# Causal attention with group norm on one core: diagonal blocks packed in pairs, with the tokens of odd blocks reversed

## The chip, the core and the metric

The kernel runs on one core of a Trainium2 chip. The metric is the device time of one execution in microseconds, which the program's own core sets. An execution is repeated, and a median is given with the lowest and highest value.

## What is computed

The input x has 32 images of 256 channels and 32 x 32 pixels. An image is treated as 1024 tokens of 256 channels. It is group normalized (32 groups of 8 channels, no scale or offset), projected to queries, keys and values, and goes through attention of 8 heads with 32 channels each; the result is added to x. The mask is strictly causal: token q sees only keys k < q, and token 0 sees none. All is float32.

```
q = q_w @ xn + q_b;  k, v = kv_w @ xn + kv_b          # xn = group_norm(x), per image
scores = q.T @ k / sqrt(32)                            # per head, 1024 x 1024
scores = where(k < q, scores, -10000)
attn = where(k < q, softmax(scores), 0)
out = x + (attn @ v).T
```

## The kernel before

**Layout.** Scores are held with keys on the 128 partitions and queries along the columns. The 1024 tokens make 8 blocks of 128. The work is done for a group g of 4 heads at a time (two groups an image) and for two halves of 512 queries. Only the blocks on and below the diagonal are computed. The exps are not divided by their sum: the value product takes the raw exps, the sums over keys are made apart, and the division comes last.

**Steps.** An image is 12 steps, 6 for each head group (`visits`). A step makes the scores of one "full" piece, 512 columns for each of 4 heads, and one "half" piece of 256 columns. The product has 32 rows (one head's channels) and 64 columns (half a block of keys), so 8 tiles of TensorE's array work beside each other (L285). The scores of a step go to three PSUM buffers `sT` of two banks each, of which the pool has three in all: two for the full piece, two heads each, and one for the half piece. ScalarE takes the exps out of them: two of 128 x 1024 into the tile `e` (L348), then one of 128 x 1024 into `eh` (L346), always in this order. The scores of the next step can begin when the exps have emptied these buffers. A piece that lies on the diagonal is masked in place by GpSimd with an affine select (L301), for 4 heads and one or two blocks at once; the half pieces of steps 0 and 5 and the full pieces of steps 0, 1, 4 and 5 lie on it. The columns above the diagonal inside a block are computed, exponentiated and then set to zero.

**What else is in a step.** After its scores a step has one projection stage for the next image (L158, into `pp` or `ppv`; L238 and L254 copy it out with ScalarE), and then the value products of the step before (L373, into `acc`). VectorE adds up the exps of all key blocks in place, for the sums over keys (L381): within one head group one 512-wide and one 1536-wide sum twice, a 2048-wide one twice, and six 1024-wide ones. Those tiles are then folded across partitions by accumulating DMAs that GpSimd issues (L397), stacked, summed and inverted, and spread again (SP's DMAs). `finish` multiplies the numerators with the inverses (L483), adds the bias and x (L484), writes token 0 (L486), and stores; it runs four times an image, in steps 1, 1, 2 and 3 of the second image after it.

**The next image.** Its norm is prepared in between. `norm_channels`, `norm_mean`, `norm_deviation` (L186 to L188, VectorE) and `norm_variance` (L200, ScalarE) come in the steps before. `norm_rstd` belongs to step 4: GpSimd makes the power −1/2 (L208) and the shift (L210). `norm_apply` (L224, ScalarE: x times rstd plus shift into `xn`, 512 columns each) comes at the end of steps 5, 6, 7 and 9. The first projection that reads `xn` comes in step 7.

**What sets the order.** The kernel runs in a manual schedule for TensorE, ScalarE, VectorE and GpSimd: each engine has its instructions in the order in which the program writes them, and the framework adds the waits. In each step the program writes the scores with their exps and masks, then what is entered for that step in `at` (projections, folds), then the value products and key sums of the step before, then what is entered in `after` (norm, finish). Two lines enter the work on the next image; the numbers are steps relative to the first step of that image:

```
PROJECT = (-5, -4, -3, -2, -1, 0, 1, 2, 3, 4, 5, 6)
PREPARE = (-16, -15, -9, -9, -8, -8, -7, -6, -5, -3)
```

The last two entries −8 of PREPARE are `norm_variance` and `norm_rstd`, and the four after them `norm_apply`. So GpSimd's queue holds, in this order: the mask of step 4, the power, the shift, the masks of step 5, a fold, and the masks of the next head group's step 0, which is step 6. ScalarE's holds: the exps of step 5, a projection's copy, the first `norm_apply`, the exps of step 6.

Of the kernel before, what the change touches and what calls it, by code (L numbers as in the profile page):

```python
# [28 lines left out]
WIDE = 64  # L29
# [3 lines left out]
def tile_norm_attention_residual(  # L33
# [65 lines left out]
    def unshifted():  # L99
# [24 lines left out]
        def load_weights():  # L124
            for n, w in enumerate((q_w, kv_w[0:C], kv_w[C : 2 * C])):
                live["wn", n] = epool.tile([P, 4, HALFBANK], F32, tag="eh", bufs=4, name=f"wn_{n}")[:, :NG, :C]
                nc.sync.dma_start(out=live["wn", n], in_=w.rearrange("(o p) c -> p o c", p=P))
# [33 lines left out]


# [49 lines left out]
        def norm_apply(b, hf, g):  # L212

            if (hf, g) == (0, 0):
                live["xn", b] = work.tile([P, NG, S], F32, tag="xn", name=f"xn_{b}")
            cols = slice(hf * HALF, (hf + 1) * HALF)
            xn, xt = live["xn", b][:, g, cols], live["x", b][:, g, cols]
            rstd = live["rstd", b][:, g : g + 1]
            if (b, hf, g) == (0, 0, 1):
                nc.scalar.activation(xn, live["less_mean"], AF.Identity, scale=rstd)  # L220
            elif b == 0:
                nc.vector.tensor_scalar(xn, xt, live["minus_mean", b][:, g : g + 1], rstd, ALU.add, ALU.mult)
            else:
                nc.scalar.activation(xn, xt, AF.Identity, bias=live["shift", b][:, g : g + 1], scale=rstd)  # L224

        def project_qk(b, g, n, hf):
# [6 lines left out]
            for cc in range(NG):  # L233
                product(
                    pp, wT[:, cc, n * C + g * P : n * C + (g + 1) * P], live["xn", b][:, cc, cols],
# [6 lines left out]
        def project_v(b, n):  # L242
# [4 lines left out]
            pp = spare(f"ppv_{b}_{n}").rearrange("p (s c) -> p s c", c=C)  # L247
            for s in range(2):
                for cc in range(NG):
                    product(  # L250
                        pp[:, s, :], live["xn", b][:, cc, (2 * n + s) * P : (2 * n + s + 1) * P],
                        wT[:, cc, 2 * C : 3 * C], start=cc == 0, stop=cc == NG - 1,
                    )
# [12 lines left out]
        def piece(g, hf, k, part=None):  # L266
            d = k - hf * BPH
            if d == 1:

                blocks = [(k, slice(P, HALF), slice(P, HALF)), (k + 2, slice(0, P), slice(3 * P, HALF))]  # L270
            elif d == 2:
                blocks = [(k, slice(0, HALFBANK), slice(HALFBANK, HALF))]
            elif part is not None:
                blocks = [(k, slice(0, HALFBANK), slice(part * HALFBANK, (part + 1) * HALFBANK))]
            else:
                blocks = [(k, slice(0, HALF), slice(0, HALF))]
            return g, hf, k, part, tuple(blocks)

        def scores_of(pc, pair, j, n=0):

            b, (g, hf, k, part, blocks) = pc
            rows = slice(HD * j, HD * (j + 1))
            kb, cols, of = blocks[n]
            return [
                nc.tensor.matmul(  # L285
                    pair[c : c + WIDE, cols], lhsT=live["k", b, g][rows, kb * P + c : kb * P + c + WIDE],
                    rhs=live["q", b, g][rows, hf * HALF + of.start : hf * HALF + of.stop],
                    start=True, stop=True, skip_group_check=True,
                )
                for c in range(0, P, WIDE)  # L290
            ]

        def mask(pc, e, heads=slice(0, 4)):


            g, hf, k, part, blocks = pc
            if k < hf * BPH:
                return
            n = len(blocks)
            diagonal = e[:, heads, : n * P].rearrange("p j (n q) -> p j n q", q=P)  # L300
            nc.gpsimd.affine_select(  # L301
                out=diagonal, in_=diagonal, pattern=[[0, heads.stop - heads.start], [0, n], [1, P]],
                compare_op=ALU.is_gt, fill=0.0, base=0, channel_multiplier=-1,
            )
            if k == 0:
                nc.gpsimd.memset(e[0:1, heads, 0:1], 1.0)

        def scores(b, full, half):


            tag = "e0" if full[2] == 0 else "e"
            name = f"{b}_{full[0]}_{full[1]}_{full[2]}"
            e = epool.tile([P, 4, HALF], F32, tag=tag, bufs=4 if tag == "e0" else 3, name=f"{tag}_{name}")
            eh = epool.tile([P, 4, HALFBANK], F32, tag="eh", bufs=4, name=f"eh_{name}")
            pairs = [ps_s.tile([P, 2, HALF], F32, tag="sT", name=f"sT_{name}_{a}") for a in range(3)]
            short = pairs[2].rearrange("p bank (n q) -> p bank n q", n=2)
            last = b == B - 1 and full[:2] == (NG - 1, NH - 1) and half[2] == NB - 2
            short_of = lambda heads, n: [m for j in heads for m in scores_of((b, half), short[:, j % 2, n, :], j)]
            long_of = lambda heads, n: [scores_of((b, full), pairs[j // 2][:, j % 2, :], j, n) for j in heads]


            if not last:
                first = short_of((2, 3), 1)
                for n in range(len(full[4])):
                    long_of(range(4), n)
            else:
# [3 lines left out]
                first = short_of((2, 3), 1)  # L330
                long_of((2, 3), 1)

            for ins in first:
                ins.then_inc(bank_free, 1)
# [470 lines left out]
```

## Time and profile before

| | |
|---|---|
| median of 3 runs | 1820.99 us (1820.59 to 1821.17) |
| profiled execution | 1821.87 us |
| its span in the profile | 1820.1 us |
| TensorE busy | 1807.9 us, 99% |
| VectorE busy | 1655.6 us, 91% |
| ScalarE busy | 1480.0 us, 81% |
| GpSimd busy | 798.9 us, 44% |
| exps L348, 128 x 1024 | 768 of 1022 ns |
| exps L346, 128 x 1024 | 384 of 1030 ns |
| `norm_apply` L224, 128 x 512 | 124 of 831 ns |
| `finish` L484, 128 x 512 | 124 of 758 ns |

The profile is one execution taken by the hardware profiler. PE is TensorE, DVE VectorE, ACT ScalarE, POOL GpSimd. A matmul of float32 is two records, since it runs in two passes. Busy times of matmuls overlap, so the starts of stages tell more than their durations. In a row of the profile, `e<-e,eh` names what is written and what is read, by the program's names, and L381 is a line of the kernel.

### The profile page before, as it was taken

What the parts mean: (1) busy time and instruction counts of PE and PEld (TensorE: products, weight loads), DVE (VectorE), ACT (ScalarE), POOL (GpSimd) and SP (SyncE); (2) the same over time, 40 slices, a digit from 0 to 9 for tenths busy, and PEclk for the clock granted to TensorE, in tenths of its full rate; (3) what the DMA queues carried; (4) which work ended last, traced back from release to release, by engine and by line L of the source; (5) the groups of instructions that cost most, each with busy time, mean ns of one, the idle gap of its engine ahead of it and who ended that gap; (6) DMA issues with size and microseconds to landing.
All of it is one profiled execution on the core that took longest, in us unless ns stands there. A gap on an engine that the chain in (4) does not pass through costs nothing. (4 is left out here: it accounts for less than half of the span.)

```text
span 1820.1 us, 68098 instructions
## 1 busy us (share of the span) xinstructions
PE 1807.9 (99%) x30388; PEld 837.4 (46%) x30388; DVE 1655.6 (91%) x1762; ACT 1480.0 (81%) x1860; POOL 798.9 (44%) x774
## 2 busy tenths in 40 slices
PE   9999999999999999999999999999999999999997
PEld 5444444444444444444444444444444444444443
DVE  4799999999999999999999999999999999999988
ACT  6888878888888888788887888877888878888885
POOL 1444544535435445344354353443444544435532
PEclk9999999999999999999999999999999999999999
DMA  3457676676776766767767667676667676676662
GB/s 123 71 98 137 134 150 113 133 148 125 147 127 125 143 128 137 148 121 133 142 129 147 116 135 150 124 141 136 123 137 136 134 152 115 129 152 124 124 124 73
DMA packets 77836, 235.91 MB, mean 130 GB/s; under 512 B 20320, under 2 KB 21344, under 8 KB 61664
## 3 DMA queue, kind: packets, MB, share of 16 engines
q0 software_dynamic: 15872, 97.53, 40.1%
q1 hardware_dynamic: 61664, 133.96, 26.4%
q8 instruction: 239, 3.92, 0.9%
q14 instruction: 61, 0.50, 0.1%
HBM read 66.85 MB, written 34.57 MB: 56 GB/s over the span
## 5 line engine op out<-in xcount | busy, mean ns | idle before, releaser
L348 ACT ACTIVATE e<-sT 128x1024 f32<-128x1024 f32 x768 | 745.2, 1022 | 269.3 <-PE sT L285 214.5
L381 DVE TENSOR_TENSOR e<-e,e 128x1536 f32<-128x1536 f32 x376 | 632.5, 1682 | 17.7
L381 DVE TENSOR_TENSOR e<-e,eh 128x1024 f32<-128x1024 f32 x380 | 524.2, 1394 | 112.3 <-PE acc L373 92.8
L301 POOL TENSOR_SCALAR_AFFINE_SELECT e<-e 128x512 f32<-128x512 f32 (+1 forms) x257 | 381.9, 1486 | 549.6 <-ACT e L348 546.4
L285 PE MATMUL sT<-q,k 32*64 32x256 f32 (+3 forms) x14336 | 601.3, 447 | 0.2
L158 PE MATMUL pp<-xn,wT 128*32 128x512 f32 x4096 | 492.4, 598 | 0.1
L285 PEld LDWEIGHTS sT<-q,k 32*64 32x64 f32 x14336 | 353.3, 130 | 212.9 <-ACT eh L346 64.7
L373 PE MATMUL acc<-e,v 128*32 128x512 f32 (+2 forms) x4096 | 400.8, 486 | 0.0
L346 ACT ACTIVATE eh<-sT 128x1024 f32<-128x1024 f32 x384 | 395.6, 1030 | 0.0
L397 POOL DMA_DIRECT2D e<-e x248 | 202.0, 824 | 399.5 <-DMA e<-e 305.3
L158 PE MATMUL ppv<-wT,xn 128*32 128x256 f32 x4096 | 247.5, 382 | 0.0
L373 PEld LDWEIGHTS acc<-e,v 128*32 128x32 f32 x4096 | 133.1, 110 | 223.1 <-issue 192.1
L373 PE MATMUL acc<-eh,v 128*32 128x256 f32 x3072 | 224.6, 379 | 0.0
L158 PEld LDWEIGHTS pp<-xn,wT 128*32 128x32 f32 x4096 | 107.5, 109 | 237.2 <-issue 228.9
L373 PEld LDWEIGHTS acc<-eh,v 128*32 128x32 f32 x3072 | 98.8, 110 | 164.0 <-issue 153.0
L158 PEld LDWEIGHTS ppv<-wT,xn 128*32 128x32 f32 x4096 | 120.3, 109 | 110.8 <-issue 44.7
L301 POOL TENSOR_SCALAR_AFFINE_SELECT eh<-eh 128x512 f32<-128x512 f32 x128 | 166.7, 1302 | 0.6 <-ACT eh L346 0.2
L224 ACT ACTIVATE xn<-x,shift,rstd 128x512 f32<-128x512 f32 x124 | 103.1, 831 | 0.0
L484 DVE SCALAR_TENSOR_TENSOR rb<-rb,v_bias_col,x 128x512 f32<-128x512 f32 x124 | 94.0, 758 | 4.4
L238 ACT ACTIVATE k<-pp,qk_bias 128x512 f32<-128x512 f32 x128 | 89.8, 702 | 2.3 <-PE pp L158 1.2
L238 ACT ACTIVATE q<-pp,qk_bias 128x512 f32<-128x512 f32 x128 | 89.9, 702 | 1.0 <-PE pp L158 1.0
L410 DVE STREAM_TRANSPOSE turned<-folded 128x512 f32<-128x512 f32 x124 | 87.6, 706 | 2.2
(70 smaller groups left out, 665.8 us busy)
## 6 DMA issues: line engine op xcount, KB each, us to landing
e<-e POOLq DMA_DIRECT2D x124, 512.0 KB, 6.8
x<-in_x_dram SPq DMA_DIRECT2D x64, 512.0 KB, 6.3
e<-e POOLq DMA_DIRECT2D x124, 256.0 KB, 4.6
folded<-e SPq DMA_DIRECT2D x124, 256.0 KB, 3.9
rb<-inverses SPq DMA_DIRECT2D x124, 256.0 KB, 8.0
out_dram<-rb SPq DMA_DIRECT2D x124, 256.0 KB, 4.7
inverses<-inv_turned SPq DMA_DIRECT2D x31, 32.0 KB, 1.7
out_dram<-rb_last SPq DMA_DIRECT2D x3, 256.0 KB, 2.5
```

The source lines that it names most:

```text
L158: nc.tensor.matmul(out[part], lhsT=lhsT[:, part], rhs=rhs, start=start, stop=stop, skip_group_check=True)
L224: nc.scalar.activation(xn, xt, AF.Identity, bias=live["shift", b][:, g : g + 1], scale=rstd)
L238: nc.scalar.activation(live[key][:, cols], pp, AF.Identity, bias=qk_bias[:, n, g : g + 1], scale=(SCALE, 1.0)[n],)
L285: nc.tensor.matmul(pair[c : c + WIDE, cols], lhsT=live["k", b, g][rows, kb * P + c : kb * P + c + WIDE], rhs=live["q", b, g][rows, hf * HA ...
L301: nc.gpsimd.affine_select(out=diagonal, in_=diagonal, pattern=[[0, heads.stop - heads.start], [0, n], [1, P]], compare_op=ALU.is_gt, fill= ...
L346: exp = nc.scalar.activation(eh.rearrange("p (n bank) q -> p bank n q", n=2), short, AF.Exp)
L348: nc.scalar.activation(e[:, 2 * a : 2 * a + 2, :], pairs[a], AF.Exp)
L373: nc.tensor.matmul(acc[HD * j : HD * (j + 1), of], lhsT=live["v", b][:, kb, h * HD : (h + 1) * HD], rhs=e[:, j, cols], start=first, stop=l ...
L381: nc.vector.tensor_add(total[:, :, of], total[:, :, of], e[:, :, cols])
L397: nc.gpsimd.dma_start(out=total[:rows], in_=total[rows : 2 * rows], accum_op=ALU.add)
L410: nc.vector.transpose(turned, live["folded", b][:, j, :])
L484: nc.vector.scalar_tensor_tensor(rb, rb, v_bias_col[:, g : g + 1], xt[:, g, cols], ALU.add, ALU.add)
```

## The change

A block on the diagonal needs only the columns q > k: the first 64 keys need 128 columns, and the last 64 keys only the last 64. The change lays two neighbouring diagonal blocks, an even one and the odd one after it, into 192 columns of scores instead of 256. Two things make that possible. The tokens of every odd block are stored in reverse order, so that its triangle is the mirror image; `norm_apply` writes `xn` so, and q, k and v follow from it. And the scores of a pair (`pair`) are made in four pieces: on the first 64 partitions 128 columns of the even block and 64 of the odd one, on the last 64 partitions 128 of the odd one and 64 of the even one.

The masks no longer work in place. For each pair two affine selects of 128 x 512 read overlapping windows of the raw exps and write the two full blocks into a tile of their own (`diagonal`, "D"), which the value products and key sums then read. Before, a head group had two selects of 128 x 1024 and four of 128 x 512; now it has eight of 128 x 512. The memset for token 0 stays.

The pieces of a head group are dealt anew to the 6 steps (VISITS): the pairs lie in the half pieces of steps 0, 4 and 5, and in the full piece of step 1. So the masks of steps 0, 4 and 5 follow the exp of `eh`, those of step 1 the exps of `e`. The exps of a step with a pair take only the columns that are used (192 instead of 256 for each head in the half pieces, 448 instead of 512 in step 1). PRODUCTS, ADDS and SUMMED list, for each step, the value products, the key sums of VectorE and what TensorE sums at the end of the last image. The sizes of the key sums in a head group are the same as before. A head group has 152 instructions for the scores where it had 112, and 76 for the values where it had 56.

`xn` is now two tiles, one for each half image, from three buffers, and each `norm_apply` is two instructions of 256 columns, one for the even and one for the odd blocks. In `finish` the product goes into `num`, and the addition is two instructions of 256 columns, the second of which reads the odd blocks backwards. The pool of `e` has four buffers instead of three, that of `eh` three instead of four. The last projection of the last image comes one step earlier (7 instead of 8). PREPARE, the folds and the place of `finish` are as before. In the changed kernel the power is L213 and the shift L215, the scores L298, the masks L324.

```diff
+        def blocks(tokens, s, turned=False):
+            of = tokens.rearrange("p (n s t) -> p n s t", s=2, t=P)[:, :, s, :]
+            return of[:, :, ::-1] if turned else of
...
         def norm_apply(b, hf, g):
-            if (hf, g) == (0, 0):
-                live["xn", b] = work.tile([P, NG, S], F32, tag="xn", name=f"xn_{b}")
+            if g == 0:
+                live["xn", b, hf] = work.tile([P, NG, HALF], F32, tag="xn", bufs=3, name=f"xn_{b}_{hf}")
...
-                nc.scalar.activation(xn, xt, AF.Identity, bias=live["shift", b][:, g : g + 1], scale=rstd)
+            for s in range(2):
+                to, of = blocks(xn, s), blocks(xt, s, s == 1)
...
+                    nc.scalar.activation(to, of, AF.Identity, bias=live["shift", b][:, g : g + 1], scale=rstd)
...
+        def pair(j, at):
+            even, odd = 2 * j, 2 * j + 1
+            c0, c1, c2, c3 = (at + n * KEYS for n in range(4))
+            return at, 3 * KEYS, [
+                [
+                    (0, even, even * P, P, slice(c1, c3)),
+                    (0, odd, odd * P, KEYS, slice(c0, c1)),
+                ],
+                [
+                    (KEYS, odd, odd * P, P, slice(c0, c2)),
+                    (KEYS, even, even * P + KEYS, KEYS, slice(c2, c3)),
+                ],
+            ]
...
-        def mask(pc, e, heads=slice(0, 4)):
-            g, hf, k, part, blocks = pc
-            if k < hf * BPH:
-                return
-            n = len(blocks)
-            diagonal = e[:, heads, : n * P].rearrange("p j (n q) -> p j n q", q=P)
-            nc.gpsimd.affine_select(
-                out=diagonal, in_=diagonal, pattern=[[0, heads.stop - heads.start], [0, n], [1, P]],
-                compare_op=ALU.is_gt, fill=0.0, base=0, channel_multiplier=-1,
+        def mask(b, g, raw, at, j):
+            hf, place = j // 2, (2 * j % 4) * P
+            if j % 2 == 0:
+                live["e", b, g, "D", hf] = epool.tile(
+                    [P, 4, HALF], F32, tag=("e0", "e")[hf], bufs=4, name=f"diagonal_{b}_{g}_{hf}"
+                )
+            square = live["e", b, g, "D", hf]
+            for s in range(2):
+                nc.gpsimd.affine_select(
+                    out=square[:, :, place + s * P : place + (s + 1) * P],
+                    in_=raw[:, :, at + (1 - s) * KEYS : at + (3 - s) * KEYS],
+                    pattern=[[0, 4], [(1, -1)[s], P]], compare_op=ALU.is_gt, fill=0.0, base=0,
+                    channel_multiplier=(-1, 1)[s],
+                )
...
-            e = epool.tile([P, 4, HALF], F32, tag=tag, bufs=4 if tag == "e0" else 3, name=f"{tag}_{name}")
-            eh = epool.tile([P, 4, HALFBANK], F32, tag="eh", bufs=4, name=f"eh_{name}")
+            e = epool.tile([P, 4, HALF], F32, tag="e0" if i == TOTAL else "e", bufs=4, name=f"e_{name}")
+            eh = epool.tile([P, 4, HALFBANK], F32, tag="eh", bufs=3, name=f"eh_{name}")
...
-            for heads in (range(2), range(2, 4)) if last else (range(4),):
-                mask(full, e, slice(heads.start, heads.stop))
-            mask(half, eh)
+            if i in PAIRS:
+                where, at = PAIRS[i]
+                mask(b, g, live["e", b, g, where, i], at, PAIRS_OF[i])
...
-            nc.vector.tensor_mul(rb, num[:, within], rb)
-            nc.vector.scalar_tensor_tensor(rb, rb, v_bias_col[:, g : g + 1], xt[:, g, cols], ALU.add, ALU.add)
+            num = num[:, within]
+            nc.vector.tensor_mul(num, num, rb)
+            for s in range(2):
+                nc.vector.scalar_tensor_tensor(
+                    blocks(rb, s), blocks(num, s, s == 1), v_bias_col[:, g : g + 1], blocks(xt[:, g, cols], s),
+                    ALU.add, ALU.add,
+                )
...
+        VISITS = [
+            ([full(0, P, 3 * P, 0), full(2, 3 * P, P, 3 * P)], [pair(0, 0)]),
+            ([full(1, 2 * P, 2 * P, 0), pair(1, 2 * P)], [full(0, 4 * P, 2 * P, 0)]),
+            ([full(1, 4 * P, 4 * P, 0)], [full(0, 6 * P, 2 * P, 0)]),
+            ([full(2, 4 * P, 4 * P, 0)], [full(5, 6 * P, 2 * P, 0)]),
+            ([full(3, 4 * P, 4 * P, 0)], [pair(2, 0)]),
+            ([full(4, 5 * P, 3 * P, 0), full(6, 7 * P, P, 3 * P)], [pair(3, 0)]),
+        ]
+        PAIRS, PAIRS_OF = {0: ("H", 0), 1: ("L", 2 * P), 4: ("H", 0), 5: ("H", 0)}, {0: 0, 1: 1, 4: 2, 5: 3}
+        ADDS = [
+            [(("L", 0, Q(2, 3)), ("L", 0, Q(3, 4)))],
+            [(("L", 0, Q(1, 3)), ("L", 1, Q(0, 2))), (("D", 0, Q(1, 4)), ("L", 0, Q(0, 3)))],
+            [(("L", 2, Q(0, 2)), ("H", 1, Q(0, 2))), (("L", 2, Q(2, 4)), ("H", 2, Q(0, 2)))],
+            [(("L", 2, Q(0, 4)), ("L", 3, Q(0, 4))), (("L", 2, Q(2, 4)), ("H", 3, Q(0, 2)))],
+            [(("L", 2, Q(0, 4)), ("L", 4, Q(0, 4))), (("L", 2, Q(0, 2)), ("D", 1, Q(0, 2)))],
...
```

## The prediction

> **What bounds the kernel now.** I read the engine shares first, then the waits of VectorE and the busy times between 400 and 1400 us (a stretch of whole images), and last the timelines of TensorE, GpSimd, VectorE and ScalarE around 600 us, where image 10 is in its steps 4 to 7. Below, 5@1.7 means 1.7 us after step 5's first score product.
>
> ```profile
> PE 1807.9 (99%) x30388; PEld 837.4 (46%) x30388; DVE 1655.6 (91%) x1762; ACT 1480.0 (81%) x1860; POOL 798.9 (44%) x774
> ```
>
> ```profile
> DVE e L381 <- PE acc L373: 35.7, 36, 1.7
> ```
>
> ```profile
> 400.00:1400.00 1000.00, 1000.00 (x16904) 461.32 (x16900) 932.68 (x982) 825.80 (x1039) 456.06 (x431) 1.00 0.70 134
> ```
>
> TensorE never pauses: 1000.00 of 1000 us, at full clock. VectorE's only wait in that stretch is for TensorE, 35.7 us in 36 waits. The stretch holds 18 images of 55.9 us, so VectorE has 35.7/18 = 1.98 us of slack an image. The timelines place it: 1.28 us in step 1, 0.66 in step 3. ScalarE's 826 of 1000 leave room. So TensorE bounds, with VectorE 3.5% behind.
>
> Timelines (start, duration, then what ran; idle time and its releaser in brackets), first TensorE:
>
> ```profile
> 596.88 1.55 PE L285 MATMUL sT<-q,k 32*64 32x256 f32 x32
> 601.62 1.59 PE L285 MATMUL sT<-q,k 32*64 32x256 f32 x48
> 603.14 1.92 PE L158 MATMUL pp<-xn,wT 128*32 128x512 f32 x16
> 606.29 1.55 PE L285 MATMUL sT<-q,k 32*64 32x256 f32 x32
> 607.76 1.92 PE L158 MATMUL pp<-xn,wT 128*32 128x512 f32 x16
> ```
>
> Steps 4, 5 and 6 begin at 596.88, 601.62 and 606.29. A score stage lasts, to the next stage, 1.47 us with 32 records and 1.52 with 48, for the same columns. Then GpSimd, VectorE, ScalarE:
>
> ```profile
> 600.08 0.67 POOL L301 TENSOR_SCALAR_AFFINE_SELECT e<-e 128x512 f32<-128x512 f32 x1 [4.76 <-ACT e L348]
> 602.11 1.45 POOL L208 TENSOR_TENSOR rstd<-rstd,power 128x2 f32<-128x2 f32 x1 [1.35 <-ACT rstd L200]
> 603.63 0.66 POOL L210 TENSOR_TENSOR shift<-mean,rstd 128x2 f32<-128x2 f32 x1
> 607.55 1.66 POOL L301 TENSOR_SCALAR_AFFINE_SELECT eh<-eh 128x512 f32<-128x512 f32 x1
> ```
>
> ```profile
> 600.23 0.54 DVE L188 TENSOR_TENSOR dev<-dev,mv 128x2 f32<-128x2 f32 x1
> 600.69 2.28 DVE L381 TENSOR_TENSOR e<-e,e 128x2048 f32<-128x2048 f32 x1
> 603.01 1.23 DVE L381 TENSOR_TENSOR e<-e,eh 128x1024 f32<-128x1024 f32 x1
> 604.34 2.29 DVE L381 TENSOR_TENSOR e<-e,e 128x2048 f32<-128x2048 f32 x1
> 606.73 1.94 DVE L381 TENSOR_TENSOR e<-e,eh 128x1024 f32<-128x1024 f32 x1
> ```
>
> ```profile
> 606.41 0.83 ACT L224 ACTIVATE xn<-x,shift,rstd 128x512 f32<-128x512 f32 x1
> 607.47 1.94 ACT L348 ACTIVATE e<-sT 128x1024 f32<-128x1024 f32 x2 [0.22 <-PE sT L285]
> 609.29 1.03 ACT L346 ACTIVATE eh<-sT 128x1024 f32<-128x1024 f32 x1
> ```
>
> A 512-wide mask takes 0.67 us alone. The one at 607.55 took 1.66: it ended at 609.21, 0.54 us after the key sum that ran until 608.67. The power at 602.11 ended at 603.56, 0.59 after the sum of 600.69; the shift at 604.29, 0.05 after the next. Each waited out a whole sum. Above all: the **shift** was ready at 604.29, 2.0 us before xn first used it (606.41).
>
> [...] a 1024-wide sum of 1.94 us instead of 1.23 behind a mask. [...] the records here stand in program order. [...] The trace has a value stage of 512 columns at 0.86 us (604.88 to 605.74) and of 384+128 at 0.87. [...]
>
> **TensorE, part by part.** A 512-column value product is two passes in 0.86 us: 0.84 ns a column and pass. A pair has 64 columns fewer: 64 x 2 x 0.84 = 0.107 us. There are 4 pairs in 6 steps and 64 half images (32 images, two head groups): 256 x 0.107 = 27.4 us less. Against it stand more pieces: five more score and five more value positions per half image (152 instead of 112 and 76 instead of 56 instructions). [...] A value position costs 0.01 us: 3.2 us. Gain **22.6 us**, from 8 to 23. Head and tail: one more 0.67 us mask behind the last exp, half-sized norm and finish pieces: +1.5 us (0.5 to 3). With TensorE bound throughout: 1821.0 − 22.6 + 1.5 = 1799.9.
>
> **ScalarE.** The narrower exps save 0.2 us in steps 0, 4, 5 and 0.1 twice in step 1 (0.82 ns a column); four norm pieces an image become eight, 0.2 us each: even, and covered by its 17% idle. The one place without cover is step 6, below.
>
> **VectorE.** L484 takes 758 ns at 512 columns, and the end's 256-wide ones 485. Two halves, the second waiting for nothing and overlapping by some 84 ns as independent neighbours do here, cost +0.13, four times an image: +0.54 us (+1.0 without overlap). The key sums keep their sizes. Masks holding it off add 0.4 us twice in step 4–5. It all lies in the 1.98 us of slack, less the 0.7 us that TensorE gets shorter. Cost 0, but the cover is nearly used up.
>
> **Buffers.** eh goes from 4 to 3, e from 3 to 4 with one more tile in it. The exp into eh of step 4 takes step 1's buffer, last read by the first 1024-wide sum of step 3's end; it was done before 598.46 (4@1.6), and the exp starts at 4@3.0. Step 5 likewise, by over 2 us. Cost 0.
>
> **GpSimd: the new stall.** Two 512-wide masks replace each 1024- or two 512-wide ones: 8 in 6 steps instead of 6. In step 4 the mask moves from behind the e exps to behind the eh exp, becomes two, and still stands ahead of the power and shift in the queue; behind these stand step 5's masks, the fold DMA of L397 and step 6's. Worked through on the trace's durations:
> - eh exp of step 4 begins at 4@3.01 as now, and at 192 of 256 columns takes 0.82 instead of 1.03: ends 4@3.83. The first mask asks at 3.90 (before: 3.20).
> - VectorE's 2048-wide sum now begins at 3.56 (dev at 3.35 now unhindered 0.16 instead of 0.54, +0.13 from L484): 0.34 us ahead of the mask. It ends 5.84; the mask 0.54 later, 6.38.
> - The 1024-wide sum gets in between (7.46); the second mask ends 8.00. The next 2048-wide sum ends 10.12; the power 0.58 later, 10.70; the last 1024-wide sum 11.45; the shift 11.50.
> - Steps 4 and 5 last 4.74 and 4.67, less 0.107 each: 9.20. So the shift is ready at **6@2.3**, where it was 2.0 us before step 6 began.
> - xn is two halves now (1.02 us until the next start): 6@2.4 to 3.4. It stands ahead of step 6's exps in ScalarE's order: two e exps at 0.915, the eh exp 0.82, ended 6.05. Three score buffers of PSUM let step 7's scores begin only then, about 0.15 later: 6@6.2 instead of 4.54.
>
> The stall is 1.65 us, in every image that prepares a next one with this order: 30. I take 1.6 (1.45 to 1.75): **+48 us**. Step 5's masks end at about 6@5.1, within the stall. The fold behind them is later by some 2 us; its sum is wanted a step later or more, so it costs 0. Sum against the profiled run: 1821.9 (span 1820.1 and 1.8 around it) − 22.6 + 1.5 + 48 = 1848.8; that run lies 0.9 above the median of 1821.0, so 1847.9: **1848**.
>
> **Rivals.**
> - *The shift is in time* (the other side). If it is ready by 6@0.65, xn, exps and eh exp still end before 6@4.4 and nothing stalls: **1800**. [...] For it: the masks alone are 0.67 each. Against: every mask and power above that met a sum waited it out.
> - *First mask wins.* If VectorE is 0.35 us later in step 4 (its slack before step 3 is 0.66, of which finish takes 0.4), the mask runs at 3.90–4.57, one sum drops out of the chain, and the shift is ready at 6@1.54: stall 0.9, 30 x 0.9 = 27: **1827**.
> - *VectorE becomes the bound.* 1.0 for finish without overlap, 0.9 for masks and 0.7 shorter images exceed 1.98 by 0.6 us: 1800 + 31 x 0.4 = **1812** or so. Nothing shown is against it but the overlap.
> - *Short passes are not shorter* (the change doesn't do what it says): if 64 columns cost what 128 do, a pair costs 256 columns as before: about **1822** without the stall, **1870** with it.
>
> **Chances.** Stall of 1.6 us 0.48, mask wins 0.12, short passes with stall 0.07, in time 0.22, VectorE 0.06, short passes alone 0.05. A measurement of this kernel tells 0.2% (3.6 us) from no change. Slower: 0.48 + 0.10 + 0.07 = 0.65 and 0.01 of the short passes, 0.66; faster 0.22 + 0.06 + 0.01 = 0.29; same 0.05. The likeliest case alone spans 1838 (gain 23, stall 43) to 1867 (gain 8, stall 53); with the other sign the range is 1798 to 1868.
>
> **What would show it.** Right: in each image the shift's record ends some 2 us into step 6, xn's wait for GpSimd shows among ScalarE's waits, and TensorE is idle about 1.6 us ahead of step 7's scores, waiting for the eh exp; its busy time over whole images falls by 0.7 us an image. Wrong: no TensorE gap at step 7, or a shift ready before step 6 begins; score stages with 64-column pieces as long as before; a VectorE without waits.

## The result, and the profile after

The changed kernel takes **1892.46 us** (median of 4 runs, 1890.76 to 1894.76) against 1821.08 us in the same comparison: a ratio of 1.0393, with a 95% interval from 1.0375 to 1.0411. It is slower by 71 us. The forecast was slower, with 1848 us and a range up to 1868: the sign and one mechanism were right, the size was not. The profiled execution has a span of 1891.0 us.

First the engine shares of the changed kernel's page, and its busy times between 400 and 1400 us (the length of the stretch, then the busy time and records of PE, PEld, DVE, ACT and POOL, and last the granted clock, the DMA share and GB/s; PEld is TensorE's weight loads):

```profile
PE 1849.1 (98%) x38068; PEld 984.1 (52%) x38068; DVE 1635.7 (86%) x1894; ACT 1451.7 (77%) x1985; POOL 943.3 (50%) x901
```

```profile
400.00:1400.00 1000.00, 984.42 (x20344) 522.00 (x20340) 888.14 (x1021) 781.62 (x1071) 515.58 (x483) 1.00 0.66 129
```

TensorE has 38068 records instead of 30388, and is busy 984 of 1000 us where it had been 1000. So it now waits, but only 16 us in 1000, and its busy time has *grown* by 41 us over the span. A busy TensorE hides part of the loss: the score stage of step 1 has 64 columns fewer for each head and takes 1.78 us instead of 1.52, and in image 12 TensorE is busy for all of those 1.78 us. Starts of stages are the better measure, and I use them below.

The waits of TensorE in the whole execution (who waited for whom: us in total, times, longest):

```profile
PE sT L298 <- issue: 14.4, 14, 2.6
PE acc L405 <- POOL diagonal L324: 8.7, 21, 0.8
```

The first is new in kind: "issue" means that the engine waited for nothing that the profile shows. The second is a wait for a mask. ScalarE, between 400 and 1400 us, shows the wait that was forecast:

```profile
ACT xn L231 <- POOL shift L215: 39.0, 17, 2.7
```

The shift holds xn up 2.3 us in every image. GpSimd's, VectorE's, ScalarE's and TensorE's timelines show the chain in image 10, whose step 4 begins at 619.67, step 5 at 624.27, step 6 at 628.93 and step 7 at 634.56:

```profile
623.60 4.33 POOL L324 TENSOR_SCALAR_AFFINE_SELECT diagonal<-eh 128x512 f32<-128x512 f32 x2 [5.69 <-ACT eh L375]
627.90 2.75 POOL L213 TENSOR_TENSOR rstd<-rstd,power 128x2 f32<-128x2 f32 x1
630.73 0.73 POOL L215 TENSOR_TENSOR shift<-mean,rstd 128x2 f32<-128x2 f32 x1
631.42 2.73 POOL L324 TENSOR_SCALAR_AFFINE_SELECT diagonal<-eh 128x512 f32<-128x512 f32 x2
```

```profile
623.58 2.29 DVE L423 TENSOR_TENSOR e<-e,e 128x2048 f32<-128x2048 f32 x1
625.90 1.54 DVE L423 TENSOR_TENSOR e<-e,eh 128x1024 f32<-128x1024 f32 x1
627.54 2.53 DVE L423 TENSOR_TENSOR e<-e,e 128x2048 f32<-128x2048 f32 x1
```

```profile
631.49 1.09 ACT L231 ACTIVATE xn<-x,shift,rstd 128x256 f32<-128x256 f32 x2 [2.66 <-POOL shift L215]
632.49 1.91 ACT L379 ACTIVATE e<-sT 128x1024 f32<-128x1024 f32 x2
634.30 0.80 ACT L375 ACTIVATE eh<-sT 128x768 f32<-128x768 f32 x1
```

```profile
633.04 0.40 PE L405 MATMUL acc<-diagonal,v 128*32 128x128 f32 x8
634.20 0.43 PE L405 MATMUL acc<-diagonal,v 128*32 128x128 f32 x8 [0.75 <-POOL diagonal L324]
634.56 2.01 PE L298 MATMUL sT<-q,k 32*64 32x256 f32 x64
```

The two masks of step 4 ask at 623.60, 0.02 us after a 2048-wide sum began, and take 4.33 us instead of 1.3. The power waits out the next 2048-wide sum, and the shift is done at 631.46, 2.5 us into step 6 (2.17 in most images). Then come step 5's masks, which end at 634.15, and TensorE's value products of step 5 stop for them: 0.75 us. Step 7's scores begin at 634.56, before the eh exp has ended (635.10); only the third group of their records, at 635.15, waited for it. (Image 10 is the worst case, since VectorE is 0.35 us later in it than elsewhere. In 28 of the 30 images that prepare a next one the sum begins 3.55 us into step 4, and the first mask asks 0.38 us after it.)

**The "issue" waits** come at the ends of images. TensorE's timeline where image 9 begins, and busy times of four stretches there (steps 10 and 11 of image 8, steps 0 and 1 of image 9):

```profile
539.15 1.21 PE L298 MATMUL sT<-q,k 32*64 32x128 f32 x34
542.30 1.03 PE L298 MATMUL sT<-q,k 32*64 32x128 f32 x30 [1.94 <-issue]
543.27 3.29 PE L158 MATMUL pp<-xn,wT 128*32 128x512 f32 x16
546.39 1.04 PE L405 MATMUL acc<-e,v 128*32 128x384 f32 x16
```

```profile
529.93:534.48 4.55, 4.55 (x84) 2.00 (x80) 4.52 (x6) 3.66 (x5) 0.62 (x1) 1.00 1.09 229
534.48:539.15 4.67, 4.67 (x124) 3.03 (x120) 4.46 (x3) 3.12 (x4) 3.72 (x3) 1.00 0.96 204
539.15:547.79 8.64, 6.70 (x116) 3.15 (x113) 5.97 (x5) 3.33 (x4) 4.66 (x6) 0.80 0.34 40
547.79:552.72 4.93, 4.93 (x116) 2.65 (x113) 0.45 (x1) 3.80 (x5) 1.69 (x3) 1.00 0.26 57
```

In the middle of a score stage TensorE stops for 1.94 us, with nothing in the profile that it waits for, and after it the projection takes 3.29 us instead of 1.92: the clock column reads 0.80 over this step. In the trace the granted clock is at half for 3.41 us there, and once more for 3.41 us in image 5. (The stops there were of 1.94 and, in image 5, 2.57 us, while one of 2.26 us, in image 28, had no half clock with it. What decides that, the trace does not show.) Ahead of it, in steps 10 and 11, the transfer engines are full (DMA column 1.09 and 0.96), and then nearly empty (0.34).

The DMA queues of the page name what is missing, first of the kernel before, then of the changed one:

```profile
q8 instruction: 239, 3.92, 0.9%
```

```profile
q8 instruction: 299, 4.90, 1.1%
```

TensorE's instructions are themselves transferred, in packets of 16384 bytes each. That the queue is TensorE's, the counts show: the changed kernel has 7680 matmuls more and as many weight loads, 15360 instructions, and the queue has 60 packets more: 256 instructions a packet, 64 bytes each. All its 38068 matmuls and as many weight loads are 76136 instructions, 297 packets of 256. In the trace one packet began at 527.70 and the next only at 539.52, when the full stretch ended, although the packets after it began at 544.40, 549.81 and 556.88. The late one took 1.31 us, and TensorE went on at 542.30; what filled the 1.5 us between its landing and that start, the trace does not show.

### The profile page after: what moved, and what is told of

Its sections match the earlier page's. It is cut to its first block, busy times and chain, and to the rows that moved or that the text cites. A ratio compares the mean times of both kernels' runs of the same rounds, so it can differ in the third digit from the quotient of the medians.

```text
span 1891.0 us, 83617 instructions
## 1 busy us (share of the span) xinstructions
PE 1849.1 (98%) x38068; PEld 984.1 (52%) x38068; DVE 1635.7 (86%) x1894; ACT 1451.7 (77%) x1985; POOL 943.3 (50%) x901
## 4 chain that ended last, share of the span: by engine, by line
PE 83%; POOL 11%; issue 3%; ACT 3%; DVE 0%; POOLq 0%
PE sT L298 28%; PE acc L405 22%; PE pp L158 21%; PE ppv L158 10%; POOL diagonal L324 8%; POOL rstd L213 3%; ACT e L379 2%; ACT eh L375 1%; PE pd L457 1%; PE busy L144 0%; POOL shift L215 0%; PE pm L158 0%; DVE rb_last L522 0%; PE pv L158 0%; DVE rb_last L510 0%
## 5 line engine op out<-in xcount | busy, mean ns | idle before, releaser
L379 ACT ACTIVATE e<-sT 128x1024 f32<-128x1024 f32 (+1 forms) x768 | 732.2, 1008 | 283.2 <-PE sT L298 282.4
L324 POOL TENSOR_SCALAR_AFFINE_SELECT diagonal<-eh 128x512 f32<-128x512 f32 x384 | 548.7, 1451 | 429.4 <-ACT eh L375 429.4
L298 PE MATMUL sT<-q,k 32*64 32x128 f32 (+2 forms) x19456 | 629.5, 364 | 14.6 <-issue 14.4
L423 DVE TENSOR_TENSOR e<-e,e 128x1024 f32<-128x1024 f32 x313 | 564.1, 1802 | 15.9 <-DVE e L423 0.5
L298 PEld LDWEIGHTS sT<-q,k 32*64 32x64 f32 x19456 | 425.9, 131 | 183.9 <-issue 52.7
L405 PE MATMUL acc<-e,v 128*32 128x512 f32 (+3 forms) x4096 | 377.3, 459 | 0.0
L375 ACT ACTIVATE eh<-sT 128x768 f32<-128x768 f32 (+1 forms) x384 | 356.7, 929 | 0.6 <-PE sT L298 0.6
L423 DVE TENSOR_TENSOR e<-e,eh 128x1024 f32<-128x1024 f32 x191 | 245.8, 1315 | 30.4 <-ACT eh L375 16.3
L231 ACT ACTIVATE xn<-x,shift,rstd 128x256 f32<-128x256 f32 x248 | 138.3, 621 | 67.1 <-POOL shift L215 67.1
L405 PE MATMUL acc<-diagonal,v 128*32 128x128 f32 x4096 | 169.4, 273 | 12.7 <-POOL diagonal L324 8.7
L423 DVE TENSOR_TENSOR e<-e,diagonal 128x1024 f32<-128x1024 f32 x125 | 165.8, 1327 | 13.4 <-DVE e L423 0.5
L324 POOL TENSOR_SCALAR_AFFINE_SELECT diagonal<-e 128x512 f32<-128x512 f32 x128 | 89.9, 726 | 133.4 <-ACT e L379 133.4
```

The lines of the kernel that those rows point to most:

```text
L231: nc.scalar.activation(to, of, AF.Identity, bias=live["shift", b][:, g : g + 1], scale=rstd)
L298: return nc.tensor.matmul(bank[c : c + KEYS, cols], lhsT=live["k", b, g][rows, kb * P + c : kb * P + c + KEYS], rhs=live["q", b, g][rows, ...
L324: nc.gpsimd.affine_select(out=square[:, :, place + s * P : place + (s + 1) * P], in_=raw[:, :, at + (1 - s) * KEYS : at + (3 - s) * KEYS], ...
L375: exp = nc.scalar.activation(eh.rearrange("p (n bank) q -> p bank n q", n=2)[:, :, :, :narrow], short[:, :, :, :narrow], AF.Exp)
L379: nc.scalar.activation(e[:, 2 * a : 2 * a + 2, :wide], pairs[a][:, :, :wide], AF.Exp)
L405: nc.tensor.matmul(acc[HD * j : HD * (j + 1), of], lhsT=live["v", b][:, kb, h * HD : (h + 1) * HD], rhs=e[:, j, :], start=first, stop=last ...
```

## The experiments

The theories. **L** is that of the prediction: the shift behind the masks. **F**: TensorE runs out of instructions where an image ends, because there are a quarter more of them and their packets queue behind full transfer engines. **O**: the score stages have become longer, because of the order in which the pieces of the two head pairs are issued. The rivals stand in the expectations.

**e1_early**: the norm one step earlier.

```diff
-        PREPARE = (-16, -15, -9, -9, -8, -8, -7, -6, -5, -3)
+        PREPARE = (-16, -15, -10, -10, -9, -9, -7, -6, -5, -3)
```

> The changed kernel with the norm of the next image prepared one step earlier (mean, deviation, variance, power and shift), so that power and shift stand ahead of step 4's masks in GpSimd's queue. Theory L (the masks ahead of the shift hold it back, each waiting out a sum of VectorE): the shift comes over 4 us before step 6 instead of 2.2 us into it, xn doesn't hold up the exps, step 5's masks end earlier, and the stretching of steps 6 and 7 (0.62 and 0.17 us in 30 images, 23 us) goes: about 1869 us. Rival F (TensorE starved of instructions is what stretches the steps, wherever they stand): within 5 us of the changed kernel's 1892. Steps 0 and 1 stay as they are in both.

1890.33 us (ratio 1.0387, 1.0362 to 1.0411). The shift came 6.8 us before step 6, and steps 6 and 7 were at 4.66 and 4.93 us, as theory L says. But step 2 was 0.64 us longer in 30 images. TensorE's waits name it:

```profile
PE pm L158 <- ACT k L245: 11.8, 30, 0.4
```

The product for the mean (pm) shares one PSUM buffer with the projections, and in step 2, whose value products are short, it met k's projection there. The trial put one wait in the place of another, so it decides nothing on the total.

**e2_before_more**: the kernel before, with more and shorter value products. (The first key block starts the sum twice here, once for each half, and the result has a relative error of 0.042; the run serves for the time alone.)

```diff
+                mid = (of.stop - of.start) // 2
+                for lo, hi in ((0, mid), (mid, 2 * mid)):
...
-                        acc[HD * j : HD * (j + 1), of], lhsT=live["v", b][:, kb, h * HD : (h + 1) * HD],
-                        rhs=e[:, j, cols], start=first, stop=last, skip_group_check=True,
+                            acc[HD * j : HD * (j + 1), of.start + lo : of.start + hi],
+                            lhsT=live["v", b][:, kb, h * HD : (h + 1) * HD],
+                            rhs=e[:, j, cols.start + lo : cols.start + hi], start=first, stop=last, skip_group_check=True,
```

> The kernel before, with every value product cut into two of half the columns: 112 instead of 56 instructions a head group, the same columns; TensorE's records rise from 30388 to about 37600, as in the changed kernel (38068). Theory F (the instruction fetch of TensorE falls behind at the end of an image, when the transfers are thick, as soon as an image has a quarter more instructions): gaps of 0.5 to 4 us at the image ends and 1845 to 1865 us. Rival (more pieces cost only their 0.01 us each): 14 x 64 x 0.01 = 9 us, 1830.

1850.18 us (ratio 1.0153, 1.0120 to 1.0185), 37556 records. The starts of the stages give the split: an undisturbed image is 0.13 us longer, 4 us in all, and the rest, some 25 us, is gaps of 0.1 to 2.6 us, nearly all in steps 0, 5 and 11. TensorE's waits now have rows of a kind that this view of the kernel before has none of:

```profile
PE acc L375 <- issue: 5.0, 5, 1.2
PE sT L285 <- issue: 4.3, 7, 1.1
PE pp L158 <- issue: 3.0, 3, 1.5
```

More instructions alone, with nothing of the change, bring the gaps: theory F. Their queue has 295 packets here, 56 more than in the kernel before, for 14336 more instructions: 256 a packet again.

**e3_order**: the score pieces of a step merged by the columns that each head pair has already been given.

```diff
-                first = short_of((2, 3))
-                for n in range(len(longs)):
-                    long_of(range(4), n)
...
+                                order.append((start, len(order), heads, bank_of, halves, n))
+                                start += halves[0][n][3]
                order.sort(key=lambda o: o[:2])
```

> The changed kernel with the score pieces of a step issued in order of the time at which each of the two head pairs can start them (a head pair's pieces one after the other, merged by columns already issued), instead of piece by piece over all four heads. The same instructions. Theory O (the two head pairs run beside each other in the array, but one waits at the head of the queue for the other when their pieces differ): step 1's score stage falls from 1.78 to about 1.4 us, those of steps 0 and 5 from 1.51 by 0.1; 0.5 to 0.6 us a head group, 64 times: 1855 to 1860 us. Rival P (a piece of 64 columns costs by itself what one of 128 costs or more): stages and time as in the changed kernel, 1892.

1900.05 us (ratio 1.0439, 1.0420 to 1.0457): worse than the changed kernel, where the theory had 1855 to 1860. The steps show two effects. Step 1 became 0.17 us shorter (4.93 to 4.76), but step 4 0.45 us longer and steps 0 and 5 0.12. In step 4 the load of the first short piece for heads 0 and 1, which waits for a semaphore of heads 2 and 3's short pieces, ran at 0.72 us into the stage in the changed kernel and at 1.37 here, although those pieces themselves ran at the same time (0.33 us in). What differs is that a 512-column piece now stood ahead of them in program order; it ended at 1.11. The semaphore itself was raised from 0.56 to 0.68 us into the stage in the changed kernel, and from 1.20 to 1.33 here. In e9 below those pieces stand in front again, the semaphore is back at 0.56 to 0.68, and step 4 at 4.56 us. So here a semaphore on a short piece came only after the longer piece ahead of it in program order had ended; whether that is so in general, these runs do not show.

**e4_nofold**: the changed kernel without the first folding transfer.

```diff
+            if rows == HD:
-            nc.gpsimd.dma_start(out=total[:rows], in_=total[rows : 2 * rows], accum_op=ALU.add)
+                nc.gpsimd.dma_start(out=total[:rows], in_=total[rows : 2 * rows], accum_op=ALU.add)
```

> The changed kernel without the first of the two folding transfers (64 rows, 512 KB each, 124 in all); half of each sum over keys is left out of the result. Theory F (instructions come late because their transfers queue behind the others): fewer and shorter gaps at image ends, 10 to 30 us less, 1862 to 1882. Rival (the gaps come from the number of instructions alone, whatever else is transferred): within 5 us of 1892.

1857.68 us (ratio 1.0198, 1.0181 to 1.0215), 35 us less and 4 under the forecast. In its trace every image from 2 to 30 has the same length within 0.2 us. Steps 6 and 7 are as long as before the edit, and "issue" is gone from TensorE's waits, which begin now with

```profile
PE acc L405 <- POOL diagonal L324: 9.8, 25, 0.4
```

**e13_before_nofold**: the same edit in the kernel before.

> The kernel before without the first folding transfer (half of each sum over keys is left out of the result): what that transfer costs where the instructions come in time. Theory F: hardly anything, 1817 to 1822 us, so that the 35 us that leaving it out saved in the changed kernel are those of the instructions. Rival (the transfer costs GpSimd or VectorE as much in any kernel): 1790 to 1800 us.

1819.77 us (ratio 0.9984, 0.9978 to 0.9991): 2.3 us less. The transfer costs nothing like 35 us where the instructions come in time, so some 33 us of the changed kernel's 71 are theory F's. The kernel before has two gaps of its own in its trace, 0.75 and 0.53 us; here they are gone.

**e6_early2**: the norm earlier, with the mean in step 1 and the power and shift in step 3.

```diff
-        PREPARE = (-16, -15, -9, -9, -8, -8, -7, -6, -5, -3)
+        PREPARE = (-16, -15, -11, -10, -9, -9, -7, -6, -5, -3)
```

> The changed kernel with the norm of the next image earlier again, placed so that none of its small products meets a PSUM buffer still in use: mean in step 1, deviation in step 2, variance, power and shift in step 3. (With everything one step earlier, the product for the mean waited 0.64 us in step 2 for ScalarE to empty that buffer, which took the place of the 0.78 us that steps 6 and 7 had lost.) Theory L: steps 6 and 7 at 4.66 and 4.93 us, no new wait in steps 1 to 3, 0.78 x 30 = 23 us less than the changed kernel: 1869. Rival F alone (the fetch of instructions takes up whatever TensorE is given): about 1885.

1874.70 us (ratio 1.0279, 1.0262 to 1.0296): 18 us less than the changed kernel, between theory L's 1869 and the rival's 1885. Steps 6 and 7 were at 4.66 and 4.93, step 1 0.04 longer. The gaps had grown by some 4 us, and step 11 had more of them.

**e7_early2_nofold**: both edits.

> The same, and without the first folding transfer (half of each sum over keys is left out of the result), which had taken the gaps of the instruction fetch away at 1857.7 us. Theory L and F together: 1857.7 - 23 = 1834 to 1835 us, and TensorE without a wait over whole images; what is left over the kernel before is the longer score stages, 0.40 us an image, 13 us. If the shift's lateness was not what stretched steps 6 and 7: 1858.

1836.72 us (ratio 1.0073, 1.0056 to 1.0090), 21.0 us less than e4_nofold. With the instructions in time, L is worth 21 us; the forecast for this run had been 23. The busy times between 400 and 1400 us have TensorE at 999.68.

**e9_all**: both, and the order mended.

```diff
-                order.sort(key=lambda o: o[:2])
+                order.sort(key=lambda o: (o[2] == (0, 1) or o[3] is long_bank, *o[:2]))
```

> The same again (norm earlier, first folding transfer left out), and the score pieces reordered: the pieces of heads 2 and 3 that come first stay in front, since the next ones for heads 0 and 1 wait for their semaphore, and only the rest is merged by columns already issued. In the first trial of an order a 512-column piece stood ahead of them, and that semaphore came 0.65 us later in step 4. Theory O, so mended: step 1's stage 0.17 us shorter as there, the others the same or 0.05 shorter: 0.17 x 64 = 11 us and up to 6 more, 1818 to 1824 us. Rival: the mended order does as badly as the first, 1835 or more.

1825.45 us (ratio 1.0017, 1.0010 to 1.0024), 11.3 us less than e7_early2_nofold and 1.5 above the forecast. Step 1 went from 4.97 to 4.80 and step 7 from 4.93 to 4.76; the others stayed. The same instructions in another order are 11 us faster: theory O.

**e10_later**: nothing left out; the inverses and their spreading transfers two steps later, finish one step later, with the norm of e6 and the order of e9.

```diff
-        FINISH = (N + 13, N + 13, N + 14, N + 15)
+        FINISH = (N + 14, N + 14, N + 15, N + 16)
...
-                    when(v + 2, lambda b=b: invert(b))
+                    when(v + (2 if late else 4), lambda b=b: invert(b))
```

> A version with nothing left out: norm earlier as above, score pieces in the mended order, and the inverses with their spreading transfers (1 MB an image) two steps later, finish one step later. In the changed kernel the 16 transfer engines are full in steps 10 and 11 (4.5 of 4.6 us) and half empty in steps 0 and 1 (2.9 and 1.9). Theory F: with the spreading moved out of steps 10 and 11 the instructions come in time: 1820 to 1830 us. If the gaps only move along: 1845 to 1855.

1904.18 us (ratio 1.0443, 1.0426 to 1.0460). The gaps in steps 11 and 0 were gone, but step 3 was 2.5 us longer in every image:

```profile
PE pv L158 <- ACT v L262: 38.0, 29, 1.3
PE acc L431 <- ACT num L440: 23.7, 30, 0.8
```

ScalarE's copy into `num` stood behind finish, since there are eight of these buffers, two images' worth, and finish now freed them a step too late. ScalarE's queue, and TensorE behind it, waited.

**e11_later**: the changed kernel, with only the inverses two steps later (the second half of that diff).

> The changed kernel with one edit: the inverses and their spreading transfers (1 MB an image) two steps later, finish where it was. Nothing is left out. (One step later, finish held its numerator buffers so long that ScalarE's copy in step 2, and TensorE behind it, lost 2.5 us an image, while the gaps at the image ends were gone.) Theory F: the gaps at the image ends go, some 33 us: 1857 to 1865 us. If finish now waits for the spread inverses: VectorE waits for a transfer in step 1 or 2, and 1880 or more.

1860.87 us (ratio 1.0213, 1.0196 to 1.0230): 31.6 us less than the changed kernel, with nothing left out. The wait for a mask is still there, and of the 14.4 us of "issue" waits of its scores 1.7 are left:

```profile
PE acc L405 <- POOL diagonal L324: 9.5, 23, 0.8
PE sT L298 <- issue: 1.7, 5, 0.5
```

The gaps in steps 0 and 11 are gone, a few in steps 1, 5 and 6 remain; steps 6 and 7 are longer as in the changed kernel. In the median image of the trace the transfer engines are busy for 0.48 of step 11 instead of all of it, and for 0.93 of step 0 instead of 0.39. Theory F is shown three ways: more instructions alone bring the gaps, fewer transfers take them away, and so do the same transfers at another time.

**e12_later_early_order**: that, with the norm of e6 and the order of e9.

> The same edit with the earlier norm and the mended order of score pieces: all three causes answered with nothing left out. Sum of the parts: 1892 - 33 (instructions) - 21 (norm) - 11 (order) = 1825 to 1830 us, as with the folding transfer left out (1825.45). If the three don't add up: 1840 or more.

1830.99 us (ratio 1.0050, 1.0033 to 1.0067). It is 1 us above the forecast. The three effects add up, but for some 6 us of gaps in steps 1, 5 and 6, which e11 has too.

**e14_unpaired1**: the same, with the pair of step 1 taken apart. (The lists of what reads its tile change with it.)

```diff
-            ([full(1, 2 * P, 2 * P, 0), pair(1, 2 * P)], [full(0, 4 * P, 2 * P, 0)]),
+            ([full(1, P, 3 * P, 0), full(3, 3 * P, P, 3 * P)], [full(0, 4 * P, 2 * P, 0)]),
...
-                    in_=raw[:, :, at + (1 - s) * KEYS : at + (3 - s) * KEYS],
+                    in_=raw[:, :, 3 * P * s : 3 * P * s + P] if j == 1 else raw[:, :, at + (1 - s) * KEYS : at + (3 - s) * KEYS],
```

> The last version (inverses later, norm earlier, order mended; 1830.99 us) with the pair of step 1 taken apart again: its two diagonal blocks as two pieces of full width, 384 and 128 columns, as in the kernel before; pairs stay in steps 0, 4 and 5, out-of-place masks everywhere. Theory: of the four pairs of a head group the one in step 1 costs more than its 64 columns bring (its stage is 0.10 to 0.14 us longer than before, those of 0, 4, 5 are 0.04 longer, 0.06 to 0.18 and 0.00 shorter): 0.24 x 32 = 8 us less, 1820 to 1824 us, the same as the kernel before, and fewer gaps of the instruction fetch. Rival (all pairs cost alike, the instructions decide): 1828 or more.

1831.44 us (ratio 1.0057, 1.0044 to 1.0069): a miss in the total. Step 7 is 4.64 us, as forecast, and no image has a gap. But step 1 is 5.09: with exps of full width, ScalarE copies q later (it ends at 4.87 us into step 1 of image 12, and at 4.52 in e12), and the product for the mean, which e6 had put there, waits for it, 30 times by TensorE's waits.

**e15_mean0**: that product in step 0.

```diff
-        PREPARE = (-16, -15, -11, -10, -9, -9, -7, -6, -5, -3)
+        PREPARE = (-16, -15, -12, -11, -9, -9, -7, -6, -5, -3)
```

> The last version (pairs in steps 0, 4 and 5 only) with the small product for the mean in step 0 instead of step 1, where it had waited 0.2 us and more for ScalarE's copy of q and lengthened step 1 to 5.09 us. Theory: step 1 at 4.64 us, as step 7 is already, 0.46 x 30 = 14 us less: 1817 to 1819 us, 0.2% under the kernel before; the fewer columns then do gain, little. Rival (another wait takes its place in step 0 or 1): 1825 or more.

1820.07 us (median of 21 runs) against 1822.39 for the kernel before (25 runs): a ratio of 0.9988, 0.9982 to 0.9995, and 1 us above the forecast. Step 1 is 4.64; step 0 took 0.12 of it back (4.78). TensorE's waits in the whole execution have only the start, the end and two of 0.4 and 0.3 us:

```profile
PE acc L431 <- issue: 0.4, 1, 0.4
PE sT L298 <- issue: 0.3, 1, 0.3
```

So the packing, in three of its four places and with everything that it disturbs put right, brings a tenth of a per cent. Whether that tenth is the packing's own is not shown: the kernel before was not run with the later inverses and the earlier norm, and taking a transfer away alone brought it as much (2.3 us, e13).

## Why the prediction was right in part and wrong in size

What an image costs, from the starts of the score stages in the traces (us; undisturbed steps, that is the tenth percentile over images, except for steps 6 and 7 of the changed kernel, which are those of most images):

```
step            0     1     4     5     6     7     10    11    image
before         4.63  4.66  4.74  4.66  4.63  4.66  4.62  4.67   55.81
changed        4.66  4.93  4.60  4.66  5.27  5.09  4.55  4.67   56.98
e7             4.66  4.97  4.57  4.66  4.66  4.93  4.55  4.67   56.21
e9             4.66  4.80  4.56  4.66  4.66  4.76  4.55  4.67   55.88
e15            4.78  4.64  4.56  4.66  4.66  4.64  4.55  4.67   55.71
(steps 2, 3, 8, 9: 4.20, 5.10, 4.20, 5.06 in all)
```

The loss of 71 us has three parts, each tried on the chip. The instructions that come late are 31.6 us (e11) to 32.5 (34.8 of e4, less 2.3 of e13). The late shift is 21.0 (e7 against e4; by the table 0.77 x 30 = 23). The longer stages of an undisturbed image are 56.21 − 55.81 = 0.40 us by 32 images, 13 us. Together that is 66 to 69 of the 71; the rest is the start and the end (some 2 us, where the forecast had 1.5) and gaps that e11 still has. By the starts of the stages in the traces the gaps sum to some 37 us in the changed kernel, 7 in e11, 0.3 in e4 and 1.6 in the kernel before.

**GpSimd's chain was right.** In 28 of 30 images the sum began at 4@3.55 and the first mask asked at 4@3.93, both within 0.03 us of the forecast. The shift was ready at 6@2.17 in most images, where the forecast had 2.3. In image 10, shown above, VectorE was 0.35 us late, and the mask missed by 0.02 us only. Why a mask waits out VectorE's sum, no run shows; that it does, the starts and ends there show (two masks in 4.33 us instead of 1.3). The rivals "in time" and "first mask wins" are out. That the late shift is the cause can also be seen inside one run, e4, whose trace has no gaps. In its image 1 no 2048-wide sum stood in the first mask's way, the shift was ready at 6@0.65, and steps 6 and 7 took 4.66 and 4.93 us. In image 2, with the shift at 6@2.17, they took 5.27 and 5.09.

**The stall from it was half of what I forecast**, 0.77 us instead of 1.6. The step that failed is "Three score buffers of PSUM let step 7's scores begin only then". They began before the eh exp ended: only their third group of records waited for it, and step 7 became 0.16 us longer. And "Step 5's masks end at about 6@5.1, within the stall" was right on the time (6@4.87 in most images, 5.22 in image 10) and wrong on the effect: the value products at the end of step 6 read these masks, and their wait, which makes step 6 0.61 us longer, comes first. I had put the masks' end beside a stall that came later, without asking who reads them.

**TensorE's gain of 22.6 us was a loss of 13.** The term that failed is the cost of the score positions. The forecast's gain has 1.6 us in it for all of them (27.4 − 3.2 − 22.6), an assumption of mine that no trace or run showed. The short pass itself is as cheap as I took it: in image 12, starts of 64-column records that follow each other lie 0.056 us apart, and of 128-column ones 0.109. But each stage with a pair should have lost 0.107 us. Those of steps 4 and 10 lost 0.06 and 0.08 (from 1.47 and 1.48 us); those of steps 0, 5, 6 and 11 changed by −0.01 to +0.03; and those of steps 1 and 7 went from 1.52 to 1.78 with 64 columns fewer. Together that is +0.42 us an image. In steps 1 and 7 the trace fits heads 0 and 1 and heads 2 and 3 running unequal pieces and waiting for each other: the same instructions in another order gave 11 us back (e9, 1.61 us), and with the pair taken apart the stage is 1.48 us (e14). Why steps 0, 5, 6 and 11 gained nothing, no run shows. The upper end of my range for this term, 16 us, was 0.05 us for each of 5 x 64 positions: what a stage of 48 records took longer than one of 32 in the trace of before (1.52 and 1.47 us). No piece of that stage was narrower than 128 columns, and the end was too low: the term was short by 22.6 + 13 = 36 us in all.

**The largest part was not in the prediction at all.** It counted "152 instead of 112" instructions, and charged them only as passes through the array. Every instruction is also some 64 bytes that TensorE has to be sent (4.90 MB in the page's queue of instructions by 76136, where it had been 3.92 MB): a packet every 6.3 us (1891 by 299) instead of 7.6. The limit could have been seen before: in the trace of before the transfer engines are full in steps 10 and 11 of the median image (1.00), but the page's slices are too long to show a step, and the prediction has no busy times of single steps. The trace of before also has gaps of this kind (a step 0 longer by 0.75 us, a step 5 by 0.53), which I did not take up. So 1892 lay outside the range: the sum of the forecast's own terms would have been 1821 + 13 + 1.5 + 23 = 1859 with the sizes set right (e4 has 1857.68), and the instructions make up the rest.

Of the signs that I had named, the shift's end and xn's wait for it came as said. The gap of 1.6 us ahead of step 7 did not, nor did a busy time that falls; and a sign of being wrong, score stages as long as before, came in six of eight stages. Three sums of the forecast do not come out, though nothing hangs on them: 1821 − 23 + 1.5 + 43 is 1842 and not 1838; the rival of VectorE finds 0.6 us too much and multiplies 0.4; and ScalarE's account, called even, saves 1.6 us an image and adds 0.8 (its busy time fell by 28 us over the span).

VectorE was no bound: between 400 and 1400 us it waited longer for TensorE, where it had waited 35.7 us before. (Its busy time there fell from 933 to 888 us, mostly because the stretch holds fewer images.)

```profile
DVE e L423 <- PE acc L405: 66.3, 35, 6.8
```

ScalarE's narrower exps into eh took 0.82 us, as forecast.

## What to carry to other kernels

Where an engine is busy all the time with small instructions, count the instructions as bytes: here the change that traded columns for more pieces took 4.90 MB of instructions instead of 3.92, and a packet of them came late behind two steps in which the transfer engines were full (1.09 and 0.96). Before moving a step behind another in an engine's queue, write down what stands behind it and who reads each of these results first, the nearest reader included. And undo causes together as well as singly: here the best single edit that left nothing out (e11) left the kernel 39 us slower than before, and three together (e12) left it 9 us slower.

## What the runs showed of the hardware that I had not expected

- TensorE ran dry of instructions where it waited for nothing else that the profile shows. With 76136 of them in 1891 us, 16 KB packets behind two full steps (about 9 us) left gaps of 0.1 to 2.6 us. Two of them, of 1.94 and 2.57 us, came with a half clock of 3.41 us, and their steps became 3.97 and 4.49 us longer; one of 2.26 us did not.
- Program order bore on score matmuls of different heads, whose records overlap (in step 0 of image 12 the first eight begin within 0.08 us and take 0.32 to 0.53 us): the same pieces in another order changed step 1 by −0.17 us and step 4 by +0.45, where a 512-column piece stood ahead of short pieces with a semaphore, which then came 0.65 us later.
- A pass of 64 columns took 0.056 us where passes followed each other directly, in proportion to one of 128 (0.109). The stages did not follow: six of eight with 64 columns fewer were not shorter by more than 0.01 us.
